# A four-layer graph network: six buffers of gathered rows in layer 0, three weights loaded with layer 1, adjacency keys in quarters of the array

## The chip, the cores and the metric

One core of a Trainium2 chip runs the whole network. Five engines work beside each other, each with its own queue of instructions in a fixed order: TensorE (PE, with weight loads listed as PEld), VectorE (DVE), ScalarE (ACT), GpSimd (POOL) and SyncE (SP). SP, ACT and POOL also issue DMA transfers, each in the order of its own queue, so a transfer whose buffer is not free holds whatever is behind it. The metric is the device time of one execution in microseconds; the program runs once and ends with its last store.

## The reference

4096 nodes with 256 values each pass through four layers. Every layer is `x = x + gnn(relu(layernorm(x)))`, and every `gnn` attends over the neighbours that a 4096 x 4096 int32 matrix `adj` names. About eight other nodes a row are set, so nearly all of the matrix is zero.

```python
h = jnp.maximum(_layernorm(x), 0.0)
# layer 0: 8 heads of 32
h = (h @ W.T).reshape(n, 8, 32)
logits = leaky_relu(e_l[:, None, :] + e_r[None, :, :], 0.2)
logits = logits + gate * einsum('ijf,hf->ijh', abs(curv[:, None] - curv[None]), Wc)
attn = softmax(where(adj > 0, logits, -1e9), axis=1)
out = einsum('ijh,jhd->ihd', attn, h)
# layer 1: one head, leaky_relu((h @ a1)[:, None] + (h @ a2)[None, :] + b_a, 0.2)
# layer 2: softmax of e and of -e, both applied to the input, then concat @ wtrans and elu
# layer 3: 4 heads, leaky_relu(h h^T, 0.01) where adj > 0, else 1.0; relu(softmax @ h)
```

`wtrans` belongs to layer 2; `W` and `b` of layer 3 are called `w3_t` and `b3` in the kernel.

## The kernel before

The kernel (`gnn_lists`) doesn't compute dense attention. In layer 0 it reads `adj` once and makes, for each of the 32 tiles of 128 rows, a list of up to nine chunks of 128 neighbours: `nbr[:, t, c]` holds row numbers. From then on each layer gathers the rows of those neighbours from a table in HBM and works on them. A second program, the dense one, runs only if the lists don't fit, and isn't run here.

**From adjacency to lists.** The matrix comes in 128 pieces of 512 KB (8 blocks `r` of 512 rows, 16 pieces `k` each, `PB = 2` blocks of 128 columns in a piece). `piece` has SP load one (L1166, five buffers) and ACT or DVE turn it into a mask in bf16 (L1169, L1171, four buffers). `pack` multiplies each 128 x 512 block of the mask by `enc`, a matrix that weighs 16 neighbouring columns by powers of two and puts the sums of its eight segments on eight of the 128 output partitions. Sixteen blocks accumulate in one bank, `kps` (L1190): with `KP = 128` output columns in each matmul, all but eight of them zero. `lift_b` (L1189) starts the bank with an offset. The result becomes keys (`key_t`), which `rank` sorts, `columns` decodes, `places` and `mark` turn into a 0/1 matrix `st` for a tile, and `find_edges` (L1421) into `nbr`. In `find_edges` each of nine chunks takes two matmuls on `st` (L1429) and one that adds the constant `edge` through `ident_b` (L1433).

**Layer 0's tiles.** `begin0` fetches `x` of tile t on SP (L890, four buffers) and has POOL issue seven indirect DMAs, one a chunk (L914), into a buffer `g`, 128 x 10 x 270 float32; `begin0_late` issues the last two chunks and, on SP, the tile's own rows (L927). Then come `before0`, `score0`, `turn_d`, `curve`, `weigh0`, `attend0` (twenty matmuls, L933, in `summed`), `finish0`, `turn1` and `rows1`, which stores the row of layer 1's table. The attend is the last to read `g`, so it frees the buffer. `g_pool` holds `G0 = 5` buffers. Its first serves weights that are folded at the start.

**The order.** TensorE's order is written out: `put(when, f, ...)` gives each step a time in a plan, and the steps are recorded sorted by it. In the plan a piece falls due every 2.5 us (`T_PIECE`), a tile every 11.5 us (`T_TILE`), so some 4.6 pieces stand between two attends, in each queue. The other engines' orders are set by a scheduler from the same steps.

**Layers 1 to 3** run in `run`: round by round, each step of a tile with its own lag. `begin` issues a tile's gathers four rounds ahead (`2 - G1`), so six buffers are needed: five of `g_pool` and a sixth of a pool `g_more`, which is made after layer 0, since layer 0's working storage leaves no room for it before. Layer 1's first gathers read rows that tiles 0 to 27 of layer 0 stored.

**Later weights.** `later_weights`, due at 70 in the plan, loads and folds what layers 1 to 3 need; among it `w3_s`, `wt_s` and `b3_s` (L1134 to L1136), 7 KB a partition that lie in `const` from the start. ACT issues these loads.

Of the kernel before, what the change touches and what calls it, by code (L numbers as in the profile page):

```python
# [9 lines left out]
F32 = mybir.dt.float32  # L10
BF16 = mybir.dt.bfloat16
I32 = mybir.dt.int32
# [3 lines left out]
OP = mybir.AluOpType  # L16
# [4 lines left out]
P = 128  # L21
C = 256
KC = C // P
# [669 lines left out]
SEG = 16  # L693
KMAX = 24
PB = 2
RG = 4 * P
EC = 9
# [2 lines left out]
KX = 8  # L700
LATE = EC - 1
EARLY = EC - 2
G0, G1 = 5, 6
ROW0, ROW1, ROW3 = C + H0 + CF, C + 2, C
LOW, HIGH = 1.0e-34, 1.0e30
FAR = 4096
# [5 lines left out]
def gnn_lists(  # L712
# [27 lines left out]
    nc = tc.nc  # L740
# [3 lines left out]
    HB = min(NB, 16)  # L744
    NH = NB // HB
    SB = P // SEG
    KP = HB * SB
    NR = N // RG
    GT = min(NT, 4)
    MID = N // 2  # L750
# [3 lines left out]
    const = ctx.enter_context(tc.tile_pool(name="const", bufs=1))  # L754
# [66 lines left out]
    inv = [const.tile([P, NT, n], F32, name=f"inv{i}") for i, n in enumerate((H0, 1, 2, K3))]  # L821
    bias1 = const.tile([P, C], F32, name="bias1")
    cst = const.tile([P, 1], F32, name="cst")
    w3_s = const.tile([P, KC, C], F32, name="w3_s")
    wt_s = const.tile([P, 2 * KC, C], F32, name="wt_s")
    b3_s = const.tile([P, C], F32, name="b3_s")
    g_pool = ctx.enter_context(tc.tile_pool(name="g", bufs=G0))
    rows12 = [const.tile([P, 2, ROW1], F32, name=f"row12_{i}") for i in range(2)]


# [113 lines left out]
    with tc.tile_pool(name="keep", bufs=1) as keep, tc.tile_pool(  # L944
        name="find", bufs=2
# [13 lines left out]
        nc.scalar.dma_start(w0_s, w0.rearrange("(k p) f -> p k f", p=P))  # L959


        enc = []
        for i in range(2):
            enc.append(keep.tile([P, HB, KP], BF16, name=f"enc{i}"))
            nc.any.memset(enc[i], 0.0)
        power = keep.tile([P, 1], I32, name="power")
        nc.vector.tensor_scalar(power, number, SEG - 1, None, op0=OP.bitwise_and)
# [3 lines left out]
        nc.vector.tensor_reduce(same, ident.rearrange("p (s c) -> p s c", c=SEG), AX.X, OP.add)  # L971
        for e, size in zip(enc, (1.0, 0.5)):
            on_blocks = bass.AP(
                tensor=e.tensor, offset=e.offset, ap=[e.ap[0], [KP + SB, HB], [1, SB]]
            )
            nc.vector.tensor_scalar(
                on_blocks, same[:, None, :].to_broadcast([P, HB, SB]), power.bitcast(F32), size,
                op0=OP.mult, op1=OP.mult,
            )
        minus_half = keep.tile([P, 1], F32, name="minus_half")  # L980
# [9 lines left out]
        )  # L990
        lift_b = keep.tile([P, KP], BF16, name="lift_b")
        nc.vector.tensor_copy(lift_b, lift.to_broadcast([P, KP]))

        off_diag = []
        for i, size in enumerate((0.5, 1.0)):
# [56 lines left out]
        def constants():  # L1052
            nc.scalar.dma_start(cv, curv.rearrange("(t p) f -> p t f", p=P))
            nc.vector.tensor_copy(own0[:, :, 0, H0:], cv)
            for h in range(NH):
                nc.vector.tensor_scalar(
                    seg_of[:, h : h + 1], number, float(h * KP), float(1 << SEG), op0=OP.add, op1=OP.mult
                )
            nc.vector.memset(bad, 0.0)

# [64 lines left out]
        def later_weights():  # L1125
            nc.scalar.dma_start(w1_s, w1.rearrange("(k p) f -> p k f", p=P))
            nc.scalar.dma_start(w2_s, w2_t.rearrange("(k p) f -> p k f", p=P))
            a1_s = load(keep, a1, "a1_s")
            a2_s = load(keep, a2, "a2_s")
            b1p_s = load(keep, b1_p, "b1p_s")  # L1130
            ba_s = load_row(keep, ba1, P, "ba_s")
            nc.scalar.dma_start(bias1, bcast_rows(b1, P, C))
            nc.scalar.dma_start(wcat1[:, :, :C], w1_t.rearrange("(k p) f -> p k f", p=P))
            nc.scalar.dma_start(w3_s, w3_t.rearrange("(k p) f -> p k f", p=P))  # L1134
            nc.scalar.dma_start(wt_s, wtrans.rearrange("(k p) f -> p k f", p=P))
            nc.scalar.dma_start(b3_s, bcast_rows(b3, P, C))  # L1136
# [24 lines left out]
        def on_dve(r, k):  # L1161
            return r < 2 and k % 2 == 0
# [17 lines left out]
                )  # L1180

        def pack(r, k):
            m = masks.pop((r, k))
            for i in range(PB):
                b = k * PB + i
                h, at = divmod(b, HB)
                if at == 0:
                    kps[h] = bank(ps_k, "kps")
                    nc.tensor.matmul(kps[h][:KP, :RG], lhsT=lift_b, rhs=ones_b, start=True, stop=False)  # L1189
                nc.tensor.matmul(  # L1190
                    kps[h][:KP, :RG], lhsT=enc[0 if on_dve(r, k) else 1][:, at, :], rhs=m[:, i, :],
                    start=False, stop=(at == HB - 1),
                )
            if (k + 1) * PB % HB == 0:
# [226 lines left out]
        def find_edges(t):  # L1421


            st, both = of0[t]["st"], of0[t].pop("list")
            K = KMAX + KX
            pe = bank(ps_t, "pt")[:, : EC * K].rearrange("p (c k) -> p c k", c=EC)
            for c in range(EC):
                for i in range(2):
                    nc.tensor.matmul(  # L1429
                        pe[:, c, :], lhsT=st[:, c * P : (c + 1) * P], rhs=both[:, i, :],  # L1430
                        start=(i == 0), stop=False,
                    )
                nc.tensor.matmul(  # L1433
                    pe[:, c, :], lhsT=ident_b, rhs=edge[:, c, :], start=False, stop=True
                )
            near = find.tile([P, EC, K], F32, name="near", bufs=1)
            nc.scalar.activation(near, pe, AF.Abs, bias=half_less, scale=1.0)
# [162 lines left out]
        nc.vector.tensor_reduce(bad_1, bad, AX.X, OP.add)  # L1600


    with tc.tile_pool(name="g_more", bufs=G1 - G0) as g_more, tc.tile_pool(
        name="work", bufs=2
    ) as work, tc.tile_pool(name="kept", bufs=1) as kept, tc.tile_pool(
        name="l_s", bufs=1, space=PSUM
    ) as ps_s, tc.tile_pool(name="l_m", bufs=1, space=PSUM) as ps_m:
        total_s = kept.tile([P, C + K3], F32, name="total_s")

        def s_chunks(st):  # L1610

# [62 lines left out]
        def run(table, width, x_of, steps, first=False, expand=False):  # L1674
# [23 lines left out]
                of[t]["all_x"] = of[four]["xs"]  # L1698

            def begin(t):  # L1700
                of[t]["g"] = gather_early(t, table, width, g_more if t % G1 >= G0 else g_pool)

            def begin_late(t):
                gather_late(t, of[t]["g"], table, width, range(EARLY, LATE if expand else EC))

            def late_lag(t):

                return (-1, -2, -2, -3, -3)[t] if t < 5 else 2 - G1

            steps = [(-3, loads), (2 - G1, begin), (late_lag, begin_late)] + [  # L1710
                (lag, lambda t, f=f: f(t, of[t])) for lag, f in steps
            ]
            rounds = {}
# [427 lines left out]
```

## Time and profile before

| | |
|---|---|
| median of 4 runs | 1619.62 us (1617.63 to 1623.6) |
| profiled execution | 1624.24 us, of which span 1622.5 us |
| busy of the span | PE 84%, DVE 70%, POOL 65%, ACT 41% |
| DMA | 338.04 MB, mean 208 GB/s |
| first and last gather of layer 0 (POOL) | 113.5 us, 520.9 us |
| first gather of layer 1 | 526.2 us |
| keys of the last block of rows | 404.3 us |
| attends of layer 0, first and last ended | 165.1 us, 547.5 us |

Three of the costliest groups of instructions (busy us, mean ns of one, then idle time of the engine before them and what ended it), over the whole span:

```profile
L1190 PE MATMUL kps<-mask,enc 128*128 128x512 bf16 x230 | 76.3, 422 | 20.4 <-ACT mask L1171 12.5
L1171 ACT ACTIVATE mask<-adj,minus_half 128x1024 bf16<-128x1024 int32 x112 | 125.5, 1143 | 31.7 <-DMA a_s<-in_a 14.7
L1508 DVE TENSOR_TENSOR g<-g,pb 128x2560 f32<-128x2560 f32 x32 | 90.1, 2815 | 4.7 <-ACT pb L1505 4.6
```

The first is the packing of adjacency blocks; 26 of its 256 matmuls are missing from the records. Matmuls overlap in the pipe, so their mean is more than each costs: 230 of 422 ns would be 97 us, but they cover 76.3. POOL's busy time counts the writing of a gather's descriptors; between two of them 0.30 us pass that belong to no other engine's work and are shown as `issue`.

### The profile page before, as it was taken

Reading aid. Unit: us, or ns where it says so; the run is one execution under the profiler, and the core shown is the slowest. Engines: PE = TensorE matmul, PEld = TensorE weight load, DVE = VectorE, ACT = ScalarE, POOL = GpSimd, SP = SyncE. Lnnn points to the kernel's source line nnn. Section 1 sums busy time; section 2 is a strip of 40 time slices with the busy share of each in tenths; the row PEclk is TensorE's granted clock in tenths of the full one; section 3 lists DMA queues with packets and bytes.
Section 4 is the critical chain, followed back from the end, with each engine's and each line's share of the span. In section 5 each row is a group of like instructions: output and inputs, shape, how many; then the busy total and the mean of one; then the engine's idle time right before and its main releaser. Section 6 shows DMA issues by size and latency. Waiting matters only on the chain.

```text
span 1622.5 us, 29055 instructions
## 1 busy us (share of the span) xinstructions
PE 1358.3 (84%) x9806; PEld 1112.3 (69%) x9840; DVE 1130.2 (70%) x3064; ACT 671.9 (41%) x1832; POOL 1061.4 (65%) x1146
## 2 busy tenths in 40 slices
PE   4774798988898659998985399999998699999996
PEld 2453566766676548887774288888886488888885
DVE  5755878889875546765653167777765499999996
ACT  3665667877443434443421044444444122221221
POOL 2026756666776757777777777777776577777730
PEclk9976988999899779998987699999999699999998
DMA  8969888898555647776776457677776556666620
GB/s 266 321 228 318 266 309 293 287 334 250 150 153 155 199 132 208 223 225 199 207 209 206 124 167 205 205 204 206 212 211 210 168 165 211 195 212 202 191 80 26
DMA packets 167342, 338.04 MB, mean 208 GB/s; under 512 B 31761, under 2 KB 103697, under 8 KB 167185
## 3 DMA queue, kind: packets, MB, share of 16 engines
q0 software_dynamic: 52224, 145.30, 33.4%
q1 hardware_dynamic: 67714, 134.54, 24.4%
q10 hardware_dynamic: 47246, 56.27, 10.0%
q8 instruction: 79, 1.29, 0.3%
q14 instruction: 79, 0.64, 0.1%
HBM read 282.22 MB, written 53.77 MB: 207 GB/s over the span
## 4 chain that ended last, share of the span: by engine, by line
PE 45%; DVE 14%; POOL 10%; DMA 9%; issue 9%; ACT 5%; DVEq 0%; ACTq 0%; POOLq 0%; SPq 0%
PE o L933 15%; PE o L1870 12%; POOL g L914 10%; DMA g<-table,nbr 6%; PE pt L1905 4%; PE pt L872 3%; DVE v L2000 2%; DVE s L2001 2%; PE pv L1996 2%; DMA adj<-in_adj_l 2%; PE s_ps L1614 2%; PE pt L863 1%; PE pe L1664 1%; PE kps L1190 1%; ACT mask L1171 1%
## 5 line engine op out<-in xcount | busy, mean ns | idle before, releaser
L914 POOL DMA_INDIRECT g<-table,nbr x1088 | 1046.0, 961 | 410.2 <-issue 313.5
L933 PE MATMUL o<-g,sw 128*128 128x257 f32 (+1 forms) x1216 | 285.0, 389 | 0.0
L933 PEld LDWEIGHTS o<-g,sw 128*128 128x128 f32 x1216 | 232.5, 193 | 35.7
L1870 PE MATMUL o<-g,sw 128*128 128x257 f32 x896 | 201.4, 382 | 39.3 <-DVE sw L1848 38.1
L1870 PEld LDWEIGHTS o<-g,sw 128*128 128x128 f32 x896 | 170.6, 191 | 64.8 <-DVE sw L1848 38.4
L933 PE MATMUL o<-g,s_f 128*128 128x264 f32 x576 | 150.9, 421 | 0.0
L933 PEld LDWEIGHTS o<-g,s_f 128*128 128x128 f32 x576 | 122.3, 212 | 26.3
L1171 ACT ACTIVATE mask<-adj,minus_half 128x1024 bf16<-128x1024 int32 x112 | 125.5, 1143 | 31.7 <-DMA a_s<-in_a 14.7
L1996 PE MATMUL pv<-parts,st 128*128 128x256 bf16 x864 | 107.5, 279 | 24.0 <-DVE v L2000 23.7
L1996 PEld LDWEIGHTS <-st 128*128 128x128 bf16 x864 | 86.5, 100 | 40.0 <-issue 28.0
L865 ACT COPY hT<-pt 128x256 f32<-128x256 f32 x128 | 47.2, 368 | 151.9 <-PE pt L863 147.2
L2004 ACT ACTIVATE s<-s 128x40 f32<-128x40 f32 x32 | 7.6, 236 | 235.1 <-DVE s L2003 235.1
L872 PE MATMUL pt<-wcat,hT 128*128 128x272 f32 (+2 forms) x384 | 92.2, 358 | 12.6 <-ACT hT L865 10.0
L2000 DVE TENSOR_TENSOR v<-pv,g 128x512 f32<-128x512 f32 (+1 forms) x160 | 90.7, 625 | 15.9 <-DMA g<-table,nbr 12.7
L2013 DVE TENSOR_TENSOR g<-g,pm 128x2560 f32<-128x2560 f32 x32 | 90.3, 2821 | 6.2 <-ACT pm L2010 5.2
L896 ACT ACTIVATE off<-place,minus 128x1152 bf16<-128x1152 f16 x64 | 80.1, 1252 | 34.1 <-DVE st L897 33.3
L1190 PE MATMUL kps<-mask,enc 128*128 128x512 bf16 x230 | 76.3, 422 | 20.4 <-ACT mask L1171 12.5
L1508 DVE TENSOR_TENSOR g<-g,pb 128x2560 f32<-128x2560 f32 x32 | 90.1, 2815 | 4.7 <-ACT pb L1505 4.6
L1614 PE MATMUL s_ps<-ident_b,st 128*128 128x128 bf16 x864 | 65.7, 223 | 25.5 <-DVE sw L1766 25.5
L1664 PEld LDWEIGHTS <-st 128*128 128x128 bf16 x768 | 77.5, 106 | 13.9 <-issue 1.6
L863 PE MATMUL pt<-ident,r 128*128 128x128 f32 x256 | 53.7, 295 | 38.5 <-DVE r L843 13.0
L872 PEld LDWEIGHTS pt<-wcat,hT 128*128 128x128 f32 x384 | 64.2, 200 | 27.1 <-ACT hT L865 14.4
(347 smaller groups left out, 2442.1 us busy)
## 6 DMA issues: line engine op xcount, KB each, us to landing
adj<-in_adj_l SPq DMA_DIRECT2D x128, 512.0 KB
g<-table,nbr POOLq DMA_INDIRECT x1088
rows_of<-st ACTq DMA_DIRECT2D x16, 832.0 KB
st<-rows_of SPq DMA_DIRECT2D x16, 832.0 KB
x<-x SPq DMA_DIRECT2D x24, 512.0 KB
st<-rows_of SPq DMA_DIRECT2D x16, 576.0 KB
table<-row ACTq DMA_DIRECT2D x32, 258.0 KB
g<-table SPq DMA_DIRECT2D x64, 129.0 KB
```

Of the source, the lines that this page charges most:

```text
L872: nc.tensor.matmul(pp, lhsT=hT[:, k, :], rhs=w[:, k, :], start=(k == 0), stop=(k == KC - 1))
L914: nc.gpsimd.indirect_dma_start(out=g[:, c, :width], out_offset=None, in_=table[: NE if c < EARLY else N, :], in_offset=bass.IndirectOffset ...
L933: nc.tensor.matmul(o, lhsT=a, rhs=b, start=(i == 0), stop=(i == len(pairs) - 1))
L1171: nc.scalar.activation(m, a, AF.Sign, bias=minus_half, scale=1.0)
L1190: nc.tensor.matmul(kps[h][:KP, :RG], lhsT=enc[0 if on_dve(r, k) else 1][:, at, :], rhs=m[:, i, :], start=False, stop=(at == HB - 1),)
L1508: nc.vector.tensor_mul(gh, gh, w[:, :, :, None].to_broadcast([P, K, H0, D0]))
L1614: nc.tensor.transpose(pt[:, c, :], st[:, c * P : (c + 1) * P], ident_b)
L1664: nc.tensor.matmul(ps, lhsT=to[:, b * P : (b + 1) * P], rhs=late_rows[:, b, i, :width], start=(b == 0 and i == 0), stop=(b == LB - 1 and i ...
L1870: nc.tensor.matmul(o, lhsT=sw[:, h, i].rearrange("p s r -> p (s r)"), rhs=g[:, c, : C + 1], start=(i == 0), stop=(i == HC + 1),)
L1996: nc.tensor.matmul(pv[:, k, :], lhsT=st[:, (a + k) * P : (a + k + 1) * P], rhs=parts[:, i, :], start=(i == 0), stop=(i == 2),)
L2000: nc.vector.tensor_mul(v[:, a : a + n, :], pv[:, :n, :], g[:, a : a + n, :C])
L2013: nc.vector.tensor_mul(gh, gh, w[:, :, :, None].to_broadcast([P, K, K3, D3]))
```

## The change

1. `G = 6` buffers of gathered rows lie in `g_pool` from the start; `g_more` is gone, and layers 1 to 3 use the same six.
2. `w3_s`, `wt_s` and `b3_s` move from `const` to `kept`, a pool that is made after layer 0. Their loads are issued by ACT between the last store of layer 1's table and layer 1's first work.
3. A key matmul has 32 output columns (`CT`) where it had 128, and writes one quarter of the bank's partitions: block `at` goes to quarter `j = at % 4`, place `q = at // 4`. `pack` does nothing for an even piece; for an odd one it issues the four blocks of both pieces, one for each quarter. `enc` shrinks from 128 x 16 x 128 to 128 x 4 x 32. The order of segments in the bank differs, so `seg_of` is computed from `js` and `qs`.
4. `find_edges` adds `edge` for all nine chunks in one matmul of 288 columns at the start instead of nine of 32.

```diff
-G0, G1 = 5, 6
+G = 6
...
-    KP = HB * SB
+    KP = P
+    CT = 32
...
-    w3_s = const.tile([P, KC, C], F32, name="w3_s")
-    wt_s = const.tile([P, 2 * KC, C], F32, name="wt_s")
-    b3_s = const.tile([P, C], F32, name="b3_s")
-    g_pool = ctx.enter_context(tc.tile_pool(name="g", bufs=G0))
+    g_pool = ctx.enter_context(tc.tile_pool(name="g", bufs=G))
...
-            enc.append(keep.tile([P, HB, KP], BF16, name=f"enc{i}"))
+            enc.append(keep.tile([P, CT // SB, CT], BF16, name=f"enc{i}"))
...
+            js, qs = (keep.tile([P, 1], I32, name=n) for n in ("js", "qs"))
+            nc.vector.tensor_scalar(js, number, 5, 3, op0=OP.logical_shift_right, op1=OP.logical_shift_left)
+            nc.vector.tensor_scalar(qs, number, 3, 3, op0=OP.logical_shift_right, op1=OP.bitwise_and)
+            seg_no = keep.tile([P, 1], F32, name="seg_no")
+            nc.vector.tensor_scalar(seg_no, qs, float(CT), None, op0=OP.mult)
...
-            nc.scalar.dma_start(w3_s, w3_t.rearrange("(k p) f -> p k f", p=P))
-            nc.scalar.dma_start(wt_s, wtrans.rearrange("(k p) f -> p k f", p=P))
-            nc.scalar.dma_start(b3_s, bcast_rows(b3, P, C))
...
         def pack(r, k):
-            m = masks.pop((r, k))
-            for i in range(PB):
-                b = k * PB + i
+            if k % 2 == 0:
+                return
+            for b in range((k - 1) * PB, (k + 1) * PB):
                 h, at = divmod(b, HB)
+                q, j = divmod(at, KP // CT)
                 if at == 0:
                     kps[h] = bank(ps_k, "kps")
                     nc.tensor.matmul(kps[h][:KP, :RG], lhsT=lift_b, rhs=ones_b, start=True, stop=False)
+                k_b, i = divmod(b, PB)
                 nc.tensor.matmul(
-                    kps[h][:KP, :RG], lhsT=enc[0 if on_dve(r, k) else 1][:, at, :], rhs=m[:, i, :],
-                    start=False, stop=(at == HB - 1),
+                    kps[h][j * CT : (j + 1) * CT, :RG], lhsT=enc[0 if on_dve(r, k_b) else 1][:, q, :],
+                    rhs=masks[r, k_b][:, i, :], start=False, stop=(at >= HB - KP // CT),
                 )
...
             pe = bank(ps_t, "pt")[:, : EC * K].rearrange("p (c k) -> p c k", c=EC)
+            nc.tensor.matmul(pe, lhsT=ident_b, rhs=edge, start=True, stop=False)
             for c in range(EC):
                 for i in range(2):
                     nc.tensor.matmul(
                         pe[:, c, :], lhsT=st[:, c * P : (c + 1) * P], rhs=both[:, i, :],
-                        start=(i == 0), stop=False,
+                        start=False, stop=(c == EC - 1 and i == 1),
                     )
-                nc.tensor.matmul(
-                    pe[:, c, :], lhsT=ident_b, rhs=edge[:, c, :], start=False, stop=True
-                )
...
-    with tc.tile_pool(name="g_more", bufs=G1 - G0) as g_more, tc.tile_pool(
-        name="work", bufs=2
-    ) as work, tc.tile_pool(name="kept", bufs=1) as kept, tc.tile_pool(
+    with tc.tile_pool(name="work", bufs=2) as work, tc.tile_pool(name="kept", bufs=1) as kept, tc.tile_pool(
...
+        w3_s = kept.tile([P, KC, C], F32, name="w3_s")
+        nc.scalar.dma_start(w3_s, w3_t.rearrange("(k p) f -> p k f", p=P))
+        wt_s = kept.tile([P, 2 * KC, C], F32, name="wt_s")
+        nc.scalar.dma_start(wt_s, wtrans.rearrange("(k p) f -> p k f", p=P))
+        b3_s = kept.tile([P, C], F32, name="b3_s")
+        nc.scalar.dma_start(b3_s, bcast_rows(b3, P, C))
...
-                of[t]["g"] = gather_early(t, table, width, g_more if t % G1 >= G0 else g_pool)
+                of[t]["g"] = gather_early(t, table, width, g_pool)
```

More of the change, by code (lines that the diff above doesn't have):

```diff
@@ L973, in gnn_lists @@
             on_blocks = bass.AP(
-                tensor=e.tensor, offset=e.offset, ap=[e.ap[0], [KP + SB, HB], [1, SB]]
+                tensor=e.tensor, offset=e.offset, ap=[e.ap[0], [CT + SB, CT // SB], [1, SB]]
             )
             nc.vector.tensor_scalar(
-                on_blocks, same[:, None, :].to_broadcast([P, HB, SB]), power.bitcast(F32), size,
+                on_blocks, same[:, None, :].to_broadcast([P, CT // SB, SB]), power.bitcast(F32), size,
                 op0=OP.mult, op1=OP.mult,
@@ L992, in gnn_lists @@
         nc.vector.tensor_copy(lift_b, lift.to_broadcast([P, KP]))
+        if HB * SB < KP:
+            of_q = lift_b.rearrange("p (j q s) -> p j q s", s=SB, j=KP // CT)
+            nc.vector.memset(of_q[:, :, HB * CT // KP :, :], 0.0)
         off_diag = []
@@ L1054, in constants @@
             nc.vector.tensor_copy(own0[:, :, 0, H0:], cv)
+            js, qs = (keep.tile([P, 1], I32, name=n) for n in ("js", "qs"))
[3 more added lines that the diff above has]
+            nc.vector.tensor_scalar(seg_no, qs, float(CT), None, op0=OP.mult)
+            nc.vector.tensor_add(seg_no, seg_no, js)
+            nc.vector.tensor_scalar(js, number, SB - 1, None, op0=OP.bitwise_and)
+            nc.vector.tensor_add(seg_no, seg_no, js)
             for h in range(NH):
                 nc.vector.tensor_scalar(
-                    seg_of[:, h : h + 1], number, float(h * KP), float(1 << SEG), op0=OP.add, op1=OP.mult
+                    seg_of[:, h : h + 1], seg_no, float(h * HB * SB), float(1 << SEG), op0=OP.add,
+                    op1=OP.mult,
                 )
@@ L1189, in pack @@
                     nc.tensor.matmul(kps[h][:KP, :RG], lhsT=lift_b, rhs=ones_b, start=True, stop=False)
+                k_b, i = divmod(b, PB)
                 nc.tensor.matmul(
-                    kps[h][:KP, :RG], lhsT=enc[0 if on_dve(r, k) else 1][:, at, :], rhs=m[:, i, :],
-                    start=False, stop=(at == HB - 1),
+                    kps[h][j * CT : (j + 1) * CT, :RG], lhsT=enc[0 if on_dve(r, k_b) else 1][:, q, :],
+                    rhs=masks[r, k_b][:, i, :], start=False, stop=(at >= HB - KP // CT),
                 )
+            del masks[r, k - 1], masks[r, k]
             if (k + 1) * PB % HB == 0:
@@ L1706, in late_lag @@
             def late_lag(t):
-                return (-1, -2, -2, -3, -3)[t] if t < 5 else 2 - G1
-            steps = [(-3, loads), (2 - G1, begin), (late_lag, begin_late)] + [
+                return (-1, -2, -2, -3, -3)[t] if t < 5 else 2 - G
+            steps = [(-3, loads), (2 - G, begin), (late_lag, begin_late)] + [
                 (lag, lambda t, f=f: f(t, of[t])) for lag, f in steps
```

## The prediction

> **What bounds the kernel now.** I read the slices first, then stretches of the span, then every place where POOL stood still, then what ended each stillness. The stretches (columns: engine busy time with instruction counts, granted TensorE clock, DMA share, GB/s):
>
> ```profile
> 0.00:113.00 113.00, 72.62 (x380) 49.54 (x387) 66.31 (x279) 58.40 (x142) 15.46 (x58) 0.93 0.86 278
> 113.00:405.00 292.00, 236.14 (x2186) 177.89 (x2213) 235.96 (x810) 210.38 (x373) 192.99 (x200) 0.86 0.87 291
> 455.00:526.00 71.00, 61.79 (x630) 50.59 (x626) 44.85 (x107) 28.43 (x82) 50.85 (x54) 0.95 0.61 164
> 526.00:1623.00 1097.00, 945.07 (x6234) 800.30 (x6233) 741.42 (x1718) 353.33 (x1186) 768.48 (x800) 0.93 0.62 185
> ```
>
> Up to 113 us no row is gathered; from 113 to 405 us the adjacency is still being read while tiles are worked; layer 1's first gather is at 526 us. From there to the end are 1097 us with 800 gathers, which nothing in the diff touches but a rotation of buffers and three loads. So only the first 526 us can change much. What times them is POOL's stream of gathers: 1088 of them,
>
> ```profile
> L914 POOL DMA_INDIRECT g<-table,nbr x1088 | 1046.0, 961 | 410.2 <-issue 313.5
> ```
>
> 0.95 us each and 0.30 us to the next, 1.25 us a gather, nine to a tile of layer 0: 11.25 us. Layer 0's 288 need 360 us; from 113.5 to the last at 520.9 plus 1.1 they took 408.5. The 48 us too many stand in eleven gaps (the bracket is POOL's idle time before the gather). Seven of them:
>
> ```profile
> 163.69 0.95 POOL L914 DMA_INDIRECT g<-table,nbr  x1 [5.04 <-PE o L933]
> 217.80 0.94 POOL L914 DMA_INDIRECT g<-table,nbr  x1 [8.55 <-ACT near L1437]
> 243.35 0.94 POOL L914 DMA_INDIRECT g<-table,nbr  x1 [3.22 <-issue]
> 270.84 0.94 POOL L914 DMA_INDIRECT g<-table,nbr  x1 [4.68 <-PE pb L1489]
> 287.51 0.94 POOL L914 DMA_INDIRECT g<-table,nbr  x1 [5.66 <-issue]
> 364.01 0.94 POOL L914 DMA_INDIRECT g<-table,nbr  x1 [5.36 <-issue]
> 379.89 0.94 POOL L914 DMA_INDIRECT g<-table,nbr  x1 [4.94 <-issue]
> ```
>
> The releaser named is often not the true one, so I set them against TensorE:
>
> ```profile
> 264.55 5.55 PE L933 MATMUL o<-g,s_f 128*128 128x264 f32 x18
> 280.84 5.93 PE L933 MATMUL o<-g,s_f 128*128 128x264 f32 x18
> ```
>
> These are the attends of tiles 7 and 8, ending at 270.1 and 286.8; 0.7 us after each, POOL goes on with tile 12 and 13, which take over their buffers of gathered rows. So it is in nine gaps (33.4 us): five buffers are too few. The two others (163.69 and 217.80, 13.6 us) come 0.7 to 0.9 us after the neighbour list of tile 4 and of tile 8 was written: lists came late. After 454.3 us POOL never waits till layer 0's last gather, so layer 0 ends by POOL.
>
> Why is a buffer late? Attends 0 to 17 end 13.9 us apart (165.1 to 401.4 us), slower than the gathers. TensorE is busy 81% of that stretch (45.27 of 50 us from 200 to 250), VectorE 81%, DMA 87%: all near full, TensorE nearest, its queue in a fixed order. Without adjacency work the attends come some 8.7 us apart (453 to 497 us).
>
> **The change, part by part.**
>
> *Six buffers from the start.* A gather of tile t waits for the attend of t-6, not t-5, one period of 13.9 us earlier. All nine buffer gaps are below that (longest 5.66 us), but they return where POOL at 11.25 stays faster than the attends: it gets one tile ahead, once. Bounds: 0 and 33.4 less nine ordinary spaces of 0.3, 30.7 us. One tile of POOL's time, 11 us, is what a buffer buys with the attends unchanged; I take 11. In layers 1 to 3 there were six already; the sixth only joins the same rotation: 0.
>
> *Keys in quarters.* 256 matmuls (16 per block of rows, twice) of 128 output columns become 256 of 32, in groups of four on different columns of the array, 64 groups, issued after every second piece. 96 pieces, 48 groups, come after 113 us. What four cost now:
>
> ```profile
> 211.90 0.38 PE L1190 MATMUL kps<-mask,enc 128*128 128x512 bf16 x1
> 212.99 0.59 PE L1190 MATMUL kps<-mask,enc 128*128 128x512 bf16 x2
> ```
>
> One takes 0.38, two 0.59: a further one costs 0.21 at the full clock, and 0.17 is the pipe running out. Over the stretch the records give 55.50 us for 170, 0.33 each, so 192 cost 62.7 us and a group 1.31. No quarter matmul is in the trace. If four run as one, three quarters go: -47 us of TensorE. If they run one after the other, 0; and if the array must also run empty at either end of a group, 48 x 2 x 0.17 = +16. The nearest row is the matmul of the same 512 columns, one for four, less one emptying a group (8 us) and two thirds of the rest for imperfect overlap: I take -26, 1.5 us a tile. What comes out of it on the path: the period can't fall below 0.87 x 13.9 = 12.1 us while the DMA engines have the same bytes, nor VectorE's 0.81 x 13.9 = 11.2, nor POOL's 11.25, and an idler TensorE is granted less clock (0.86 here, with 81% busy; 0.62 from 550 to 600 us, with 45%). I count half, 0.8 us a period, 17 periods: -14 us. Pairing makes an even piece's mask wait for the odd one's; four mask buffers are then two pairs. ScalarE, which makes them, would have its queue (casts of s_f, hT) stand behind a mask that finds no buffer. In this stretch its masks wait for the adjacency DMA 6.3 us in all and for no buffer worth listing: 0, and 2.5 us (one piece) a pair if that cover went.
>
> The Trainium skill, "TensorE: Matmul & The Clock Gate", section "Measured speedup vs the span model", has three column-quarters of 512 elements at 2.38 times; by it I estimate a group at 1.31/3 = 0.44 us and the gain at -42 us of TensorE, against my -26. The skill's "TensorEngine Tiling (Array Packing)", "Key Properties" and "Gotcha 2", speaks against: changing the tiling mode drains the array, and column tiling gives up the fast weight load; by that alone the sum is the +16 above. No run yet shows either.
>
> *Edge offsets in one matmul.* In a tile's find_edges, nine chunks, each two matmuls on st and one on ident_b, take 0.66 us (start 228.83, last start 229.49). A third goes (0.22) and a 288-wide one comes (about 0.12 at 0.21 for 512): -0.1 us a tile, 2 us of TensorE, inside the half above: 0.
>
> *Three weights loaded later.* 896 KB leave the first 113 us, where DMA is at 0.86 and 278 GB/s: at most 3.2 us earlier lists, at least 0; I take 2. Three issues (0.33 to 0.46 us each) go on ScalarE's queue behind the last store of table1 and ahead of layer 1's late_rows casts and marks. Their storage is layer 0's, so the first also waits for layer 0's last stores; the longest wait of a queue for an x store is 8.2 us. Cost up to 9.6 us on ScalarE, and TensorE's L1650 waits for those casts. It is hidden by
>
> ```profile
> 583.26 0.21 ACT L1764 ACTIVATE w<-s 128x10 f32<-128x10 f32 x1 [16.87 <-DVE s L1737]
> ```
>
> 16.87 us in which ScalarE waits for layer 1's first gathered rows. Cost 0; without cover 9.6. The 0.9 MB beside gathers there (DMA share 0.53): 0. Constants on VectorE: seven more of about 0.15 us, two memsets of 0.91 us shortened: 0.
>
> **Sum.** -11 - 14 - 2 = -27, of 47 us in gaps. The profiled execution took 1624.24 (span 1622.5), 4.6 above the median of 1619.62. So 1597 for that one; against the median 1593, and I say 1594.
>
> **The rivals.**
> *Only the buffer pays (1607).* The quarters overlap badly, or the clock takes it back: -11 - 2. For it: DMA at 0.87 and VectorE at 0.81 leave little room. Against: TensorE is the fullest.
> *POOL never waits (1574).* All 47 less eleven spaces of 0.3, and 2: -46. For: lists and attends both hang on TensorE's fixed order. Against: DMA must carry the same adjacency in 40 us less.
> *No change (1620).* The sixth buffer is not what is missing: SP's fetch of x, with four buffers, holds the adjacency loads behind it,
>
> ```profile
> SPq L890 <- DMA x<-x: 96.4, 17, 8.2
> ```
>
> and it is not changed. Lists then come no earlier, and gaps like that at 217.80 replace the nine. Against: only two gaps of eleven were lists, and by 400 us the loads are done.
> *Slower (1638).* One mechanism, at L1190: a quarter's weight load can't run behind a matmul and nothing overlaps: 4 x (0.106 load + 0.38) = 1.94 us a group for 1.31, 48 x 0.63 = +30 on the fullest engine, all on the path, less 13: +18. It decides from 1.31 + 13/48 = 1.58 us a group. For: emptying and no quarter seen in this trace. Against: 32 columns are less to load.
>
> **How the numbers follow.** Forecast 0.45; only the buffer 0.20; POOL never waits 0.13; no change 0.08; slower 0.14. A measurement of this kernel can tell 0.3% (4.9 us) from nothing. Faster 0.45 + 0.20 + 0.13 = 0.78, same 0.08, slower 0.14. The range 1574 to 1618 holds the forecast, the buffer alone, most of no waiting, and a part of no change; its own range for the forecast is 1584 to 1603.
>
> **What would show it.** Gaps on POOL from 113 to 526 us: 47 us before, about 22 after, the first layer 1 gather at about 500 us, and 1097 us from there to the end. A group of four at L1190 starting within 0.2 us, not 0.64. Attends 13.1 us apart. ScalarE's three issues inside its wait. Wrong if the group takes over 1.3 us, if POOL's gaps come from lists, or if the stretch after layer 1's first gather is not 1097 within 5 us.

## The result, and the profile after

The changed kernel takes 1619.66 us (median of 34 runs), the kernel before 1620.51 (55 runs beside them): ratio 0.9999, 95% interval 0.9991 to 1.0007. No change, where 1594 was forecast. Its profiled execution took 1621.22 us, with a span of 1619.5.

The two stretches that the prediction rested on, now of the kernel after (columns as before: PE, PEld, DVE, ACT, POOL busy with counts, granted clock, DMA share, GB/s):

```profile
113.00:405.00 292.00, 224.38 (x1972) 166.32 (x1981) 227.63 (x799) 203.99 (x358) 197.10 (x205) 0.77 0.88 293
526.00:1620.00 1094.00, 937.05 (x6221) 794.77 (x6219) 735.78 (x1717) 353.36 (x1183) 766.91 (x800) 0.93 0.63 186
```

From layer 1's first gather (525.1 us) to the end are 1094 us, 1097 before: nothing is hidden there. In the first stretch TensorE is busy 11.8 us less (236.14 before), but its granted clock is 0.77 where it was 0.86, and VectorE and ScalarE got less done as well. The groups of TensorE in this stretch show both sides:

```profile
L1202 PE MATMUL kps<-mask,enc 128*32 128x512 bf16 x188 | 23.7, 453 | 7.8 <-ACT mask L1180 2.9 <-DVE mask L1186 2.5 <-issue 1.1
L931 PE MATMUL o<-g,s_f 128*128 128x264 f32 x307 | 88.4, 451 | 0.0
```

In the kernel before, the same two groups were:

```profile
L1190 PE MATMUL kps<-mask,enc 128*128 128x512 bf16 x170 | 55.5, 419 | 8.3 <-ACT mask L1171 3.6 <-DVE mask L1177 2.3 <-issue 1.4
L933 PE MATMUL o<-g,s_f 128*128 128x264 f32 x324 | 84.7, 420 | 0.0
```

The key matmuls cover 23.7 us where they covered 55.5: the quarters do overlap. The attend's matmuls became slower: 307 cover 88.4 us, 0.288 each, where 324 covered 84.7, 0.261 each; their mean went from 420 to 451 ns.

POOL's long gaps before layer 1's first gather, after:

```profile
215.12 0.95 POOL L912 DMA_INDIRECT g<-table,nbr  x1 [9.75 <-PE pb L1478]
265.75 0.95 POOL L912 DMA_INDIRECT g<-table,nbr  x1 [5.18 <-ACT near L1448]
318.60 0.95 POOL L912 DMA_INDIRECT g<-table,nbr  x1 [7.41 <-PE pt L1222]
368.49 0.95 POOL L912 DMA_INDIRECT g<-table,nbr  x1 [4.81 <-issue]
384.94 0.95 POOL L912 DMA_INDIRECT g<-table,nbr  x1 [5.48 <-issue]
411.82 0.95 POOL L912 DMA_INDIRECT g<-table,nbr  x1 [3.84 <-issue]
425.99 0.95 POOL L912 DMA_INDIRECT g<-table,nbr  x1 [2.99 <-issue]
525.13 0.95 POOL L912 DMA_INDIRECT g<-table,nbr  x1 [7.65 <-PE o L931]
```

The first three come 0.83 us after the lists of tiles 8, 12 and 16 were written (214.3, 264.9, 317.8 us); the next four 0.75 us after the attend of six tiles earlier. With one more list gap (1.93 us at 159.76), lists hold 24.3 us and buffers 17.1; before it was 13.6 and 33.4. So the sixth buffer took 16 us of gaps away, and lists put 11 back. Not all of these lists come later than before: those of tiles 8 and 12 were written at 217.0 and 266.2 us there, that of tile 16 at 314.3. POOL, which no longer stops for a buffer, reaches the lists of tiles 12 and 16 before they are there. The gap at layer 1's start grew from 4.14 to 7.65.

The same in milestones, one profiled execution of each kernel (us). "Keys" is the time from the first gather until the keys of the last block of rows are written (the end of DVE's last `key_t`; in the kernel before that instruction starts at 404.3 and ends at 405.0), "tail" from there to layer 1's first gather, "rest" from there to the end of the span:

| kernel | first gather | keys | tail | layer 1's first gather | rest |
|---|---|---|---|---|---|
| before | 113.5 | 291.5 | 121.2 | 526.2 | 1096.3 |
| after | 112.0 | 302.3 | 110.8 | 525.1 | 1094.4 |

The tail is 10.4 us shorter: by then the adjacency is done, POOL sets the pace, and one more buffer means that it is a tile further on, of 11.25 us. The keys are 10.8 us slower. The one is paid by the other, almost to the microsecond. One execution can lie 4 to 5 us off its kernel's median (the profiled one of the kernel before 4.6 above), so differences of that size between milestones mean little.

### The profile page after: what moved, and what is told of

It is laid out like the page before. It is cut to its first block, busy times and chain, and to the rows that moved or that the text cites. A ratio compares the mean times of both kernels' runs of the same rounds, so it can differ in the third digit from the quotient of the medians.

```text
span 1619.5 us, 28596 instructions
## 1 busy us (share of the span) xinstructions
PE 1341.9 (83%) x9569; PEld 1096.3 (68%) x9584; DVE 1125.0 (69%) x3071; ACT 673.4 (42%) x1832; POOL 1061.9 (66%) x1145
## 4 chain that ended last, share of the span: by engine, by line
PE 42%; DVE 16%; POOL 12%; issue 11%; DMA 9%; ACT 3%; DVEq 0%; ACTq 0%; SPq 0%; POOLq 0%
PE o L931 15%; POOL g L912 12%; PE o L1885 11%; DMA g<-table,nbr 8%; PE pt L1920 3%; DVE v L2015 3%; DVE s L2016 3%; PE pt L870 3%; PE pv L2011 2%; PE s_ps L1629 1%; DVE g L1519 1%; PE pt L861 1%; PE pe L1679 1%; PE pb L1506 1%; PE pt L1907 1%
## 5 line engine op out<-in xcount | busy, mean ns | idle before, releaser
L931 PE MATMUL o<-g,s_f 128*128 128x264 f32 x576 | 155.0, 429 | 0.0
L931 PEld LDWEIGHTS o<-g,s_f 128*128 128x128 f32 x576 | 125.7, 218 | 27.8
L2011 PEld LDWEIGHTS <-st 128*128 128x128 bf16 x864 | 86.0, 100 | 41.3 <-issue 29.7
L861 PE MATMUL pt<-ident,r 128*128 128x128 f32 x256 | 55.5, 302 | 39.5 <-DVE r L841 13.3
L1679 PEld LDWEIGHTS <-st 128*128 128x128 bf16 x768 | 78.0, 106 | 13.5 <-issue 1.6
L1629 PEld LDWEIGHTS <-st 128*128 128x128 bf16 x864 | 56.0, 100 | 38.9 <-DVE sw L1781 23.4
```

Of the source, the lines that this page charges most:

```text
L931: nc.tensor.matmul(o, lhsT=a, rhs=b, start=(i == 0), stop=(i == len(pairs) - 1))
L1629: nc.tensor.transpose(pt[:, c, :], st[:, c * P : (c + 1) * P], ident_b)
L1679: nc.tensor.matmul(ps, lhsT=to[:, b * P : (b + 1) * P], rhs=late_rows[:, b, i, :width], start=(b == 0 and i == 0), stop=(b == LB - 1 and i ...
L2011: nc.tensor.matmul(pv[:, k, :], lhsT=st[:, (a + k) * P : (a + k + 1) * P], rhs=parts[:, i, :], start=(i == 0), stop=(i == 2),)
```

## The experiments

Three accounts stood against each other at first: that SP's queue (fetches of x, full adjacency buffers) brings the lists late; that an idler TensorE is granted less clock, so that the time saved comes back; and that the five-buffer limit had been the whole gain. Each kernel below is the kernel after with one edit, unless told otherwise. Ratios are to the kernel before on the same chip.

**More buffers of x; more buffers of adjacency.**

```diff
-            of0[t]["x"] = fetch(work, tile_rows(x_in, t), [P, C], "x", bufs=4)
+            of0[t]["x"] = fetch(work, tile_rows(x_in, t), [P, C], "x", bufs=7)
```

> The changed kernel with seven buffers for x in layer 0 where it had four, so that SP's fetch of x no longer waits for the store of an earlier tile (57.4 us in all from 113 to 405 us in the changed kernel). Queue theory (adjacency loads stand on SP's queue behind waits that hang on the attends): keys of the last block of rows 10 to 25 us earlier than 414 us, run 10 to 25 us faster than before. DMA theory (the engines, 0.88 busy, already carry what they can): adjacency at the same pace, within 5 us of before. Clock theory (TensorE sets the pace, and the throttle, 0.77 after 0.86, took back what the quarters saved): within 5 us of before.

Measured: 0.9977 [0.9959, 0.9994], some 3.7 us faster: within 5 us, not 10 to 25.

```diff
-            a = find.tile([P, PB, RG], I32, name="adj", bufs=5)
+            a = find.tile([P, PB, RG], I32, name="adj", bufs=6)
```

> The changed kernel with six buffers for adjacency pieces where it had five. Queue theory: one more piece is under way when SP stands still, 3 to 10 us faster than before. DMA theory and clock theory: within 5 us of before.

Measured: 0.9979 [0.9962, 0.9997], some 3.4 us, which fits either forecast. Neither gives back the 10.8 us: the keys take 299.1 us with seven buffers of x and 303.2 with six of adjacency. The queue of SP is a small part of it at most.

**Work for TensorE that computes nothing.** Ahead of each group of four quarters come three matmuls of full width with zeros as weights, into the same bank.

```diff
+            zero_b = keep.tile([P, KP], BF16, name="zero_b")
+            nc.vector.memset(zero_b, 0.0)
...
+                if j == 0:
+                    for _ in range(3):
+                        nc.tensor.matmul(
+                            kps[h][:KP, :RG], lhsT=zero_b, rhs=ones_b, start=False, stop=False
+                        )
```

> The changed kernel with three full-width matmuls of zero weights added to each group of four quarter matmuls, so that TensorE has the work of the kernel before again (192 more matmuls, sums unchanged); everything else as after the change. Clock theory, or any in which TensorE's saved time reached the path: slower by 15 us or more. Queue and DMA theories: within 5 us of before, and the granted clock from 113 to 405 us back from 0.77 towards 0.86.

Measured: 0.9956 [0.9934, 0.9977]. TensorE got more to do, and the kernel is 7 us faster, which none of the forecasts had. In the stretch from 113 to 405 us of this kernel the clock is back above where it was before:

```profile
113.00:405.00 292.00, 244.47 (x2171) 169.34 (x2199) 237.26 (x814) 210.46 (x370) 203.84 (x210) 0.87 0.90 297
```

and the attend's matmuls, in the groups of the same stretch, are short again (406 ns, 420 before the change):

```profile
L931 PE MATMUL o<-g,s_f 128*128 128x264 f32 x324 | 80.8, 406 | 0.0
L1205 PE MATMUL kps<-ones_b,zero_b 128*128 128x512 bf16 x125 | 40.4, 429 | 3.4 <-issue 2.4
```

The keys take 292.5 us, nearly as before the change (291.5), and the tail stays short (111.4). That looked like the clock's doing, but the edit changed more than TensorE's work: the orders of ACT, DVE and SP, which a scheduler sets, came out otherwise too (of the 393 transfers that SP issues, 27 stand elsewhere than in the kernel after). The two had to be parted.

**Twice the load.** Six zero matmuls a group instead of three.

> The changed kernel with six zero-weight full-width matmuls a group instead of three (TensorE has more work than before the change, 1.3 us a group). Clock theory: the clock rises little more (above 0.87), and the added work of some 30 us on TensorE starts to cost: between 8 us faster and 5 us slower than before. If TensorE's work were simply on the path: 10 us or more slower than with three.

Measured: 0.997 [0.9949, 0.9991], with a clock of 0.95 and keys in 293.1 us: 5 us faster than before, inside the range of the clock theory, though the clock rose more than it said. More load, with more clock than before the change, brings nothing further.

**Load without the order, order without the load.** In the first, the orders of ACT, DVE and SP are held to those of the kernel after, by an ordering edge between each instruction and the next of its engine; in the second, the kernel after without zeros, they are held to those of the kernel with three zeros.

```diff
+            for engine, ranks in zip((nc.scalar.engine, nc.vector.engine, nc.sync.engine), ORDER):
+                made = [i for i in nc.cur_bb.bb.instructions if i.engine == engine and ...]
+                for k in range(1, len(ranks)):
+                    tc.add_manual_dep(made[ranks[k]], made[ranks[k - 1]].name, ...)
```

> The changed kernel with the three zero-weight full-width matmuls a group, and with the orders of ScalarE, VectorE and SyncE held exactly as the changed kernel has them (a scheduler that sees the added matmuls places other instructions differently, which was so in the run with the load alone). Clock theory (TensorE's granted clock fell from 0.86 to 0.77 with the quarters, and the fixed chain of TensorE's other work is what the slower clock lengthens): clock 0.84 or more from 113 to 405 us, and 4 to 8 us faster than before. Order theory (the added load made the scheduler place adjacency and list work better): within 3 us of before, or slower.

Measured: 1.0027 [1.0005, 1.0048], 4 us slower, as the order theory had it and not the clock theory.

> The changed kernel without any added matmul, with ScalarE, VectorE and SyncE held in the orders that they had in the run with the load. Clock theory: clock 0.77 again from 113 to 405 us, time within 3 us of before. Order theory: 4 to 8 us faster than before at that same clock.

Measured: 0.9987 [0.9968, 1.0007], 2 us faster, as the clock theory had it and not the order theory: neither holds in both runs. The stretch from 113 to 405 us, first of the load with the old order:

```profile
113.00:405.00 292.00, 246.87 (x2112) 166.71 (x2112) 229.08 (x798) 203.99 (x357) 198.74 (x204) 0.84 0.89 293
```

then of the new order without load:

```profile
113.00:405.00 292.00, 230.00 (x2007) 169.93 (x2005) 229.46 (x790) 202.81 (x359) 198.17 (x204) 0.78 0.89 292
```

With the clock at 0.84 and the old order the keys take 301.9 us, with the new order at 0.78 they take 299.9; with both, 292.5. So the load, with the clock that it brings, buys nothing in the old order, and the order alone next to nothing. What more clock would do without more work was not tested, nor what holding the order costs by itself: the kernel after, held to its own order, was not run. VectorE shows it at a glance: 229 us busy in both, 237 where both come together.

**Five buffers with all the rest of the change.**

```diff
-G = 6
+G0, G = 5, 6
...
+    with tc.tile_pool(name="g_more", bufs=G - G0) as g_more, ...
```

> The changed kernel with five buffers of gathered rows in layer 0 again and the sixth from layer 1 on, so quarters, edge matmul and later loads alone. If the sixth buffer gave its 11 us and something else in the change took them back: slower than before by 8 us or more. If lists, not buffers, hold POOL (queue and DMA theories): within 5 us of before.

Measured: 1.0025 [1.0011, 1.0039]: quarters, edge and late weights without the buffer are slower than before, by 4 us, which is the second forecast. The tail is 117.8 us, the keys 299.2. Beside the kernel after, the buffer is worth 7 us of tail here, and 4 us of the time (1.0025 against 0.9999).

**Full width again.** The kernel after, its six buffers, edge and late weights kept, with keys of 128 output columns. So that six buffers find room, `enc` is one strip of zeros with the eight weights in its middle, and each block takes a window of it.

```diff
-            enc.append(keep.tile([P, CT // SB, CT], BF16, name=f"enc{i}"))
+            enc.append(keep.tile([P, 2 * KP], BF16, name=f"enc{i}"))
...
-            if k % 2 == 0:
-                return
-            for b in range((k - 1) * PB, (k + 1) * PB):
+            m = masks.pop((r, k))
+            for i in range(PB):
+                b = k * PB + i
...
-                    kps[h][j * CT : (j + 1) * CT, :RG], lhsT=enc[0 if on_dve(r, k_b) else 1][:, q, :],
-                    rhs=masks[r, k_b][:, i, :], start=False, stop=(at >= HB - KP // CT),
+                    kps[h][:KP, :RG], lhsT=e[:, KP - at * SB : 2 * KP - at * SB], rhs=m[:, i, :],
+                    start=False, stop=(at == HB - 1),
```

> The changed kernel with the quarters undone: 128 output columns a matmul, per piece, the weights taken from a strip of zeros at a sliding offset so that the six buffers still fit; buffers, edge matmul and later loads as changed. Clock theory: clock 0.84 or more, 5 to 10 us faster than before, so the quarters cost what the buffer gave. If the quarters helped by themselves: slower than the changed kernel, that is 3 us or more slower than before.

Measured: 0.9915 [0.989, 0.994], 1605.5 us, 14 us faster than before where 5 to 10 were expected. Its stretch from 113 to 405 us:

```profile
113.00:405.00 292.00, 241.37 (x2070) 180.02 (x2070) 237.11 (x809) 205.18 (x369) 203.96 (x210) 0.87 0.88 296
```

and the same two groups there:

```profile
L931 PE MATMUL o<-g,s_f 128*128 128x264 f32 x342 | 90.4, 424 | 0.0
L1189 PE MATMUL kps<-mask,enc 128*128 128x512 bf16 x184 | 56.3, 409 | 2.5 <-DVE mask L1174 2.0 <-ACT mask L1168 0.4
```

33 us more of key matmuls than after, and by the ratios 14 us less time. Keys 289.3 us, tail 113.7. On POOL the gap of tile 12's list is gone, and that of tile 16's has shrunk from 7.41 to 3.18 (list at 303.4):

```profile
208.47 0.94 POOL L912 DMA_INDIRECT g<-table,nbr  x1 [9.62 <-ACT near L1434]
304.27 0.94 POOL L912 DMA_INDIRECT g<-table,nbr  x1 [3.18 <-PE pt L1208]
369.20 0.94 POOL L912 DMA_INDIRECT g<-table,nbr  x1 [6.11 <-issue]
```

**Pairs or quarters?** The change did two things to the keys: quarters, and packing two pieces at a time. Full width in pairs, and quarters piece by piece (no early return, two blocks a call), part them.

```diff
-            if k % 2 == 0:
-                return
-            for b in range((k - 1) * PB, (k + 1) * PB):
+            for b in range(k * PB, (k + 1) * PB):
...
-            del masks[r, k - 1], masks[r, k]
+            del masks[r, k]
```

> Full-width keys in pairs of pieces. On a chip at 1620 us: pairing theory within 4 us of before, although the clock is 0.84 or more; quarter theory 8 us or more faster than before.

Measured: 0.9908 [0.9889, 0.9927], 15 us faster, as the quarter theory had it.

> Quarters, packed piece by piece. On a chip at 1620 us: pairing theory 8 us or more faster than before with the clock from 113 to 405 us below 0.83; quarter theory within 4 us of before.

Measured: 0.9975 [0.996, 0.999], 4 us faster with a clock of 0.79, at the edge of what the quarter theory allowed.

| | piece by piece | in pairs |
|---|---|---|
| full width | 0.9915 | 0.9908 |
| quarters | 0.9975 | 0.9999 (the change) |

It is the quarters: 0.6% (10 us) piece by piece, 0.9% (15 us) in pairs. The two kernels of this experiment ran on one chip (1617.69 and 1607.31 us); the other two ratios come from other chips. Quarters without added load were slow in five kernels with six buffers (0.9975 to 0.9999), one of them held to the order of the loaded kernel; full width was fast in both of its kernels. But every kernel has an order that the scheduler made for it, and full width held to an order of the quarters was not run, so the cost is that of quarters with the orders that came with them. Pairs cost nothing at full width, and with quarters perhaps 4 us, an effect whose intervals all but touch.

**The same on a slower chip.** Eight runs fell on chips on which the kernel before itself takes 2236 to 2275 us: the two kernels of the last experiment, repeated; the full-width kernel, with four and with seven buffers of x; and the change with six mask buffers instead of four. Their expectations stand in the order in which the kernels ran: full width in pairs, quarters piece by piece, six mask buffers; then full width in pairs, quarters piece by piece, full width, seven buffers of x; last, quarters piece by piece.

> Full-width key matmuls as in the run with the quarters undone, which was 0.9915 of before, but issued in pairs of pieces as the change does. Pairing theory (an even piece's mask, and through the mask and adjacency buffers the next loads, wait for the odd piece): the gain is gone, within 4 us of before. Quarter theory (the narrow matmuls cost by themselves, by a lower granted clock or by switching the array): still 10 us or more faster than before.

> The changed kernel with quarters, but packed piece by piece as before the change (two quarters at a time instead of four). Pairing theory: 10 us or more faster than before, with the clock from 113 to 405 us below 0.82. Quarter theory: within 4 us of before.

> The changed kernel, pairs and quarters, with six mask buffers where it had four. Pairing theory, if it acts through the mask buffers: 6 us or more faster than before. If it acts only through TensorE's order, or if quarters are the cause: within 4 us of before.

> The kernel of e9_wide_pairs again (full-width keys in pairs of pieces), since the chip of that call took 2236 us for the kernel before. On a chip at 1620 us: pairing theory within 4 us of before; quarter theory 10 us or more faster than before.

> The kernel of e10_quarters_single again (quarters, packed piece by piece). On a chip at 1620 us: pairing theory 10 us or more faster than before, at a granted clock below 0.82 from 113 to 405 us; quarter theory within 4 us of before.

> The kernel of e7_wide again (full-width keys, piece by piece; 0.9915 of before), beside the two above on one chip. Both theories: 10 to 17 us faster than before.

> The kernel of f3_wide with seven buffers for x in layer 0 instead of four. With them the changed kernel was 0.9977 of before where it was 0.9999 without. If the wait of SP's queue for stores of x holds adjacency: 3 to 8 us faster than f3_wide. If the DMA engines or VectorE hold the pace by now: within 3 us of f3_wide.

> The changed kernel with quarters, but packed piece by piece as before the change (two quarters at a time), for a chip at 1620 us. Full-width keys piece by piece were 0.9915 of before there. Pairing theory (issuing four blocks after every second piece is what costs): 10 us or more faster than before although the clock from 113 to 405 us stays below 0.82. Quarter theory (the narrow matmuls and the lower clock cost): within 4 us of before.

| kernel | ratios there |
|---|---|
| full width in pairs | 0.9985 [0.9957, 1.0012], 0.9979 [0.995, 1.0007] |
| quarters piece by piece | 0.9957 [0.9931, 0.9983], 0.9965 [0.9943, 0.9986], 0.9969 [0.9943, 0.9996] |
| full width | 0.9969 [0.9945, 0.9992] |
| full width, seven buffers of x | 0.9967 [0.9947, 0.9987] |
| the change, six mask buffers | 1.0012 [0.9985, 1.0039] |

There quarters show no loss against full width piece by piece. Pairs lean towards a small loss (0.9979 to 1.0012, against 0.9957 to 0.9969 piece by piece), and full width in pairs stays 3 to 5 us faster than before, nearer to the pairing theory's forecasts than to the quarter theory's; but the intervals of both overlap, so neither is shown there. Full width gained 7 us where 10 to 17 were expected, and by the ratios seven buffers of x changed nothing, as the forecast of "within 3 us" had it. In the stretch from 113 to 580 us of full width in pairs the last column reads 183 GB/s, where the same kernel's stretch from 113 to 405 us has 297 on the usual chips:

```profile
113.00:580.00 467.00, 282.62 (x1983) 196.27 (x1982) 231.76 (x794) 204.73 (x356) 194.38 (x204) 0.71 0.59 183
```

TensorE is busy 61% of the time there, where it was 83% on the usual chips; that its work therefore costs nothing there is a reading, not a test. Six mask buffers were tried only there, so whether a mask without a buffer matters on the other chip stays open.

Milestones on the usual chips; the last column adds up POOL's gaps of over 1 us between layer 0's first and last gather:

| kernel | first gather | keys | tail | keys + tail | clock, 113 to 405 us | POOL's gaps |
|---|---|---|---|---|---|---|
| before | 113.5 | 291.5 | 121.2 | 412.7 | 0.86 | 46.0 |
| after | 112.0 | 302.3 | 110.8 | 413.1 | 0.77 | 41.4 |
| five buffers | 109.5 | 299.2 | 117.8 | 417.0 | 0.77 | 52.1 |
| quarters piece by piece | 111.6 | 298.9 | 112.0 | 410.9 | 0.79 | 38.8 |
| load, old order | 111.6 | 301.9 | 111.1 | 413.0 | 0.84 | 38.9 |
| new order, no load | 106.3 | 299.9 | 112.1 | 412.0 | 0.78 | 40.3 |
| load, own order | 111.4 | 292.5 | 111.4 | 403.9 | 0.87 | 30.9 |
| double load | 107.3 | 293.1 | 111.6 | 404.7 | 0.95 | 34.3 |
| full width | 104.8 | 289.3 | 113.7 | 403.0 | 0.87 | 30.6 |
| full width in pairs | 108.7 | 292.0 | 111.4 | 403.4 | 0.86 | 30.9 |

The tail parts by buffers (118 to 121 us with five, 111 to 114 with six). The keys part in two: 299 to 303 us for quarters (303.2 with six buffers of adjacency), 289 to 293 for full width, the kernel before included, or for quarters with load and an order made for it. POOL's gaps say the same: with six buffers 39 to 41 us in the slow kernels of the table, 31 to 34 in the fast ones. The first gather, from 104.8 to 113.5, follows neither; it is one execution of each.

## Why the prediction was wrong

- **The step that failed** is "I count half, 0.8 us a period, 17 periods: -14 us." Its sign was wrong: quarters cost 10 to 15 us. What led to it was, if anything, too small: TensorE is the fullest engine, and its work on keys fell by 32 us in the records, by 39 us over all 48 groups (1.31 to 0.50 us each), where 26 were counted. But fullest is not the same as last. With full-width keys put back, TensorE has 17 us more of busy time in the stretch, and, counted from the first gather, the lists of tiles 12 and 16 come 4 and 7 us earlier (149.1 and 198.6 us, after the change 152.9 and 205.8).
- **Size of the quarters.** I took a group at 0.77 us (1.31 less 26 us over 48 groups); the 188 records cover 23.7 us, 0.50 a group. Timeline of TensorE, after:

```profile
229.25 0.40 PE L1202 MATMUL kps<-mask,enc 128*32 128x512 bf16 x4
229.59 0.44 PE L1222 MATMUL pt<-ident,key_t 128*128 128x128 f32 x2
231.09 0.40 PE L1202 MATMUL kps<-mask,enc 128*32 128x512 bf16 x4
231.42 0.83 PE L1474 MATMUL pb<-own,st 128*128 128x14 bf16 x27
```

  Four quarters take 0.40 us, where one full-width matmul took 0.38. The four start within 0.01 us of each other. The next instruction starts 0.34 us after the group, and a further matmul of 512 columns needed 0.21: at most 0.13 us a group for changing the tiling back, 6 us over 47 groups; what changing it ahead of a group costs does not show here. The rival "slower" needed a group above 1.58 us, so its mechanism falls, though it had the sign of what quarters do. The Trainium skill's "TensorE: Matmul & The Clock Gate", section "Measured speedup vs the span model", whose 2.38 times for three column-quarters I had weighed and passed over, was nearer: 1.31 to 0.50 is 2.6 times for four.
- **"An idler TensorE is granted less clock"** was written down, and priced only as a limit on the gain. The clock went from 0.86 to 0.77 in the stretch; 324 attend matmuls at 0.027 us more each are 8.7 of the 32 us, and busy time fell by only 11.8. The same page, section "HAM oscillation — how this bites in real kernels", says that idle gaps of more than some 3.4 us throttle the clock again. This case's records agree in direction: from 113 to 405 us TensorE stands still that long five times after the change, twice before. Its busy share alone doesn't tell the clock: quarters piece by piece kept it busy 236.38 us, as before the change, at 0.79. Yet the clock is not the whole cause, as the load with the old order shows.
- **Six buffers, -11.** 10.4 us of tail and 16 us of buffer gaps went, so the stage is as predicted; but beside the quarters the run with five buffers puts the sixth at 4 us of the time, and no five-buffer kernel was run at full width. The rival "only the buffer pays", 1607 us, is what the kernel becomes without quarters: 1605.5 in one form, 1607.3 in the other. These 14 us include edge and late weights (predicted 0 and -2); neither was tried alone.
- **Three weights later, -2 and no cost at the boundary.** In keeping with the runs: from layer 1's first gather to the end 1092 to 1098 us in all of them on the usual chips, and a first gather at 104.8 to 112.0 us in eleven kernels with late loads, at 113.5 before. In the kernel after, ScalarE's three issues stand at 548.6 to 550.3 us, ahead of the casts of `late_rows`, and its wait for layer 1's rows that follows is 20.07 us, so their cost stays covered.
- **"No change (1620)" by SP's fetch of x** gave the right time, and its sign, list gaps in the place of buffer gaps, came. Its cause did not: with seven buffers of x the keys still take 299.1 us.
- **What I looked for.** Gaps of 22 us, from 47, were 41, and 49 with the one ahead of layer 1's first gather (7.65), which came before 526 us this time; attends 13.1 us apart were 14.4 (13.9 before); the first layer 1 gather at 500 us was at 525. "Wrong if ... POOL's gaps come from lists" is what came true, for 24.3 of the 41 us.

What stays open is how quarters slow the keys when they free TensorE. Load and order together undo about half of it in the medians, either alone does not, which points to how the queues in fixed order meet; that isn't shown, and the scheduler's orders of ACT, DVE and SP are not the same from one of these kernels to the next. Which instructions stand in the wrong place was not found. That quarters with load (0.9956) stay behind full width in pairs (0.9908), when their stages differ by 0.5 us in one execution of each, is in part the execution: the loaded kernel's profiled one (1610.46 us) was 4 us below its median, that of full width in pairs (1607.96) at its own.

The version to keep is full width with the other parts of the change: 1605.5 us piece by piece, 1607.3 in pairs, 14 to 15 us faster than the kernel before on the same chips.

## What to carry to other kernels

Work taken from the busiest engine is worth only what the step that comes last waits for it; ask for the chain from that step (here a list, written some 50 us after its keys) before counting a share of busy time as gain. Where taking work from TensorE lowers its granted clock, as here from 0.86 to 0.77, the work comes back in part as slower work, so compare the same matmul's duration before and after. And where a scheduler sets the other engines' orders, a changed instruction on one engine is also a new order on the others: part the two by holding the order fixed.

## What the runs showed of the hardware

Matmuls with zeros as weights, 40 us of them, made the kernel 7 us faster than the same kernel without them, in an order made for them: granted clock 0.77 to 0.87, attend matmuls 451 to 406 ns. Four column-quarters of 512 bf16 columns took 0.40 us together. And the kernel before took 2236 to 2275 us on some chips, where others took 1620 to 1624, the first 113 us at the same speed (276 GB/s against 278): times from different chips don't compare, and an effect on one chip need not show on another.
